# A four-layer graph network on one core: the identity moved into the adjacency, layernorm's last step and three other steps moved

## The chip, the cores and the metric

The kernel runs on one core of a Trainium2 chip. The time is the device time of one execution in microseconds; the runs of a kernel are given by their median. A core has a matrix engine (TensorE, PE in the profile, with its weight loads as PEld), a vector engine (VectorE, DVE), a scalar engine (ScalarE, ACT), a general one (GpSimd, POOL) and a queue engine that starts transfers (SyncE, SP). Each takes its instructions in order and waits for others by semaphores. ScalarE and GpSimd can start transfers too.

## The reference

`x` is 8 batches of 2048 nodes with 64 features, `adj` a 2048 x 2048 matrix of zeros and ones with ones on its diagonal. Four layers follow each other, each adds its input and normalizes:

```python
x = layernorm(x + hypergraph_attention(x, H, adj, ...))     # layer 0
x = layernorm(x + W1 . (dinv * (adj + I) * dinv) . x)       # layer 1
x = layernorm(x + chebyshev(x, E, adj, ...))                # layer 2: u1 = adj.x, u2 = adj.u1, u3 = softmax(relu(E.E^T)).x
x = layernorm(x + 3 steps of relu([v, adj.v].W31 + b31).W32 + b32)   # layer 3, on adj
```

Layer 1 alone uses `adj + I`, with `dinv` the inverse root of its row sums. `layernorm(r) = (r - mean) / sqrt(var + 1e-5)` over 64 features. E is the table of node embeddings, 2048 x 16.

## The kernel before

Two batches of 64 features make a pair of 128 columns: 4 pairs `p`, 16 node tiles `t` of 128, 4 chunks `c` of 512 nodes. The adjacency, transposed, stays in SBUF for the whole kernel as `adj[t][g]`, 16 row tiles in two column halves, in a rounded float type (fp32r) whose matmul takes one pass over 512 columns. A product with it takes `x` in two parts, a rounded one and the rest (`split`, line 161, makes `v0h`, `v0l` to `v3h`, `v3l` by chunk): 16 tiles x 2 parts x 4 chunks = 128 wide matmuls for a pair.

TensorE's order is written out by hand: `mm` and `transpose` pin each of its instructions (lines 170 to 174). The other engines' orders come from a scheduler that follows estimated times, so that an instruction issued earlier in the code can stand later in its engine's queue. Long products are generators, and `fill(n)` (line 370) takes n of their matmuls and puts them between the steps of a loop that has waits of its own. `later(n, f)` puts `f` on a list, and `tick()`, called once for each such matmul, runs it after n of them; the list is emptied from the front only.

The stages, in order: layer 0's prologue and attention, to about 230 us; its mixing loop (16 iterations over pairs and chunks: `mix_load`, `mix_ind`, `mix_g`, `mix_scores`, `mix_weigh`, `mix_end`), filled first with layer 0's products (`products`, tile `ug`), then with layer 1's (`layer1`, tile `u`); the rest of layer 1, which is `make_el` with the embedding's transposed table and plain product; the softmax support (`apt_tile`, tile `ua`) to about 805 us; layer 2's products and its weights (`py`) to about 1508 us; layer 3.

What the change and the steps of the prediction touch:

- `layernorm` (line 133): squares on ScalarE (line 148), a sum on VectorE (150), `var + eps` (152), the power on GpSimd (154), the last multiplication on VectorE (155).
- `mix_ind`: `pi` on TensorE, then `ind = pi * inv` on VectorE (line 809). `mix_scores`: four matmuls `pf` from `ind` and `gt`, four tanh on ScalarE (837), two differences on VectorE (839). `mix_weigh`: `pd`, a tanh, `ind` (851). `mix_end`: four transposes `pt`, the sum `r` (859), layernorm, a store to `x1_hbm` (863); then, for the first pair, the start of layer 1's parts.
- `mix_g` also loads `x` and adds it on GpSimd (line 825).
- `l1_parts` (line 868): loads `x1`, scales on GpSimd (870), splits. `l1_end` (line 873): `po`, `r = po * dinv` (880), `r += x1` on GpSimd (881), layernorm, and a store to `x2_hbm` (886) or, for the last pair, straight into `xn[3]`.
- `layer1`: beside each wide matmul on the chunk that holds tile `t`'s own nodes, one of 128 columns with the identity (`ident_r`) as its right-hand side adds the `I` of `adj + I`.
- `load_emb`, `make_el`, `make_er` (lines 979 to 1006): chunks of E in staged buffers `x` of which there are two, a plain product `pb`, and the rounded `el` and `er`.
- `first` (line 1230): for layer 3, transposes `x` into `h` (line 1211) and at once multiplies it by weights (`pr`) and splits it (`factor`).
- `finish` (line 1305): layer 3's last product `po`, the residual (1310), layernorm, two stores to the output (1313). Its layernorm keeps the squares in the `x` buffers, which `r` also uses.
- `check` (line 1327): in layer 3, 64 times a 128 x 512 piece of `adj` is loaded again into `fcav`, rounded on ScalarE (1330) and compared on VectorE (1331), to tell whether rounding changed anything. The next load waits for the comparison.

Of the kernel before, what the change touches and what calls it, by code (L numbers as in the profile page):

```python
# [56 lines left out]
def tile_gnn_fast(  # L57
# [23 lines left out]
    nc = tc.nc  # L81
# [51 lines left out]
    def layernorm(pool, r, dst, groups=2 * JT, centred=False, small=None, tag="ln_c", bufs=1):  # L133
# [21 lines left out]
        nc.vector.tensor_tensor(dst, xc, rstd[:, :, None].to_broadcast([P, groups, F]), ALU.mult)  # L155
# [38 lines left out]
    wrong = const.tile([P, 6], F32, name="wrong")  # L194
# [17 lines left out]
    def adj_c(t, c):  # L212

        return adj[t][c // 2][:, cols(c % 2)]

# [68 lines left out]

    places = {}
# [11 lines left out]
    def products():  # L297
# [40 lines left out]
        for p in range(NP):  # L338
            for g in range(2):
# [4 lines left out]
                for t in range(NT):  # L344
                    for i in range(2):
                        for c in own:
# [3 lines left out]
                            )  # L350
                            if t > 1:
                                next(turning, None)
# [3 lines left out]
                    if p + 1 < NP and t % JT == JT - 1:  # L356
# [3 lines left out]
                        if g == 1 and c < 2 or g == 0 and c >= 2:  # L360
                            fetch(p + 1, (c + 2) % NCH)
                for c in own:
# [399 lines left out]
    pending = []  # L762

    def later(n, f):

        pending.append([n, f])

    def tick():
        for e in pending:
            e[0] -= 1  # L770
        while pending and pending[0][0] <= 0:
            pending.pop(0)[1]()

# [19 lines left out]
    xn, done = [], [0] * NP  # L793
# [59 lines left out]
    def mix_end(i):  # L853
# [8 lines left out]
        layernorm(mp, grouped(r), grouped(r))  # L862
        nc.sync.dma_start(x1_hbm[p][:, wide(c), :], r)
        if p == 0:
            first_parts(c, mixed)

    def l1_parts(p, c):
        y = staged("y")
# [4 lines left out]
    def l1_end(p, c, ut):  # L873
# [8 lines left out]
        if p == NP - 1:  # L882
            layernorm(lp, grouped(r), grouped(xn[p][:, wide(c), :]), centred=True)
        else:
            layernorm(lp, grouped(r), grouped(r), centred=True)
            nc.sync.dma_start(x2_hbm[p][:, wide(c), :], r)
        done[p] += 1
        load_xn()
# [8 lines left out]
    def layer1(p):  # L897

        for g in range(2):
            own = (2 * g, 2 * g + 1)  # L900
            ug = None
            for t in range(NT):
# [5 lines left out]
                for i in range(2):  # L908
                    for c in own:
                        end = t == NT - 1 and i == 1  # L910
                        half = part[p, t // JT][i][:, t % JT, :]
                        mm(
                            u[c], lhsT=half, rhs=adj_c(t, c),
                            start=t == 0 and i == 0, stop=end and t // JT != c,
                        )
# [28 lines left out]
    for i in range(steps + 1):  # L944
        k = 10 if i > NCH else 8
# [17 lines left out]
    load_xn()  # L963
# [20 lines left out]
    def load_emb(c):  # L984

        et = flat_x("et")
# [3 lines left out]
    ets = [load_emb(c) for c in range(2)]  # L990

    def make_el(c):
        et = ets.pop(0)
# [11 lines left out]
        if c + 2 < NCH:  # L1005
            ets.append(load_emb(c + 2))

    for c in range(NCH):
# [46 lines left out]
    for i, (c, t) in enumerate(order_ct):  # L1055
# [4 lines left out]
        for p in range(NP):  # L1060
# [3 lines left out]
            if t == NT - 1 and p % 2:  # L1064
                for q in (p - 1, p):
# [3 lines left out]
                    else:  # L1069
                        nc.scalar.copy(raws[c, q], ug[p // 2][:, q % 2, :])  # L1070
        if t == 1 and c > 0:
            apt_end(c - 1)
        if t == 8 and c + 1 < NCH:
            make_er(c + 1, load_emb(c + 1))
# [155 lines left out]
    def first(c, where):  # L1230
        h[c] = first_h(0, c, l2.tile([P, C], F32, tag=f"{where}{c}", name=f"h{c}"))
        factor(c, h[c], bd_e, None)
# [4 lines left out]
    for p in range(NP):  # L1237
        for c in range(NCH):
            r = staged("r").rearrange("p t (b f) -> p t b f", f=F)
            for b in range(2):  # L1240
                a_z = xg[b]
                for j in range(JT):
# [27 lines left out]
    for c in (2, 3):  # L1270
        first(c, "g")
# [33 lines left out]
    def finish(p, c, h):  # L1305
# [13 lines left out]
    left = l2.tile([P, NT, NCH], F32, tag="m", name="left")  # L1319
# [830 lines left out]
```

## Time and profile before

| what | value |
|---|---|
| median of 3 runs | 1989.77 us (1988.22 to 1994.02) |
| the profiled execution | 1991.48 us |
| its span, first to last instruction | 1989.7 us |
| mean granted TensorE clock | 0.98 |
| TensorE busy, 300 to 400 us | 93.10 of 100 |
| TensorE busy, 400 to 500 us | 87.88 of 100 |
| TensorE busy, 500 to 600 us | 90.16 of 100 |
| TensorE busy, 600 to 1400 us | 99.4 to 100 of each 100 |
| TensorE busy, 1900 to 1990 us | 72.23 of 90 |
| VectorE, GpSimd busy, 300 to 400 us | 53.46 and 43.22 of 100 |

A page of the profile gives each engine's busy time, the span in 40 slices, the chain of work that ended last and the costliest groups of instructions. In the groups, `u<-adj,v0h` is a tile written and the tiles read, followed by the shapes. In the order of time, a row is the start in us, the duration, the engine, the line, the operation, the tiles and the count; in brackets is how long the engine had stood idle before it and what ended that. Times of matmuls overlap, since the array takes the next while one ends. A wide product with fp32r operands is one record, a plain fp32 matmul two.

### The profile page before, as it was taken

The numbers are of one execution on the slowest core, as the hardware profiler recorded it, in microseconds if no ns is written. First come the engines' busy times: TensorE is split into PE (matmuls) and PEld (weight loads), VectorE is DVE, ScalarE is ACT, GpSimd is POOL, SyncE is SP. The second block draws the span as 40 slices with busy tenths as digits, with TensorE's granted clock in tenths as the row PEclk, the third lists the DMA queues.
The fourth block names the chain that finished last, engine by engine and source line by source line (L and its number), as shares of the span: only waits on it lengthen the run. The fifth ranks groups of instructions, "written<-read, shape, count | busy, mean of one in ns | idle before, by whom it ended". The sixth has DMA issues, their size and how long they took to land.

```text
span 1989.7 us, 19780 instructions
## 1 busy us (share of the span) xinstructions
PE 1887.9 (95%) x7228; PEld 1230.2 (62%) x7228; DVE 978.2 (49%) x1660; ACT 397.0 (20%) x771; POOL 519.8 (26%) x464
## 2 busy tenths in 40 slices
PE   6889899889899999999999999999999999999996
PEld 4667566556654444755665575565446777877775
DVE  6679555555422211357556736655784342332422
ACT  1445343333222111100000000000002221212211
POOL 3678643544354344311001101100001020100101
PEclk9899899989999999999999999999999999999998
DMA  9833334332400000311101110110101121211201
GB/s 310 292 105 100 130 122 143 117 110 84 154 16 27 4 24 21 118 37 53 51 35 43 56 50 32 58 49 33 46 25 40 38 64 43 59 43 48 54 22 23
DMA packets 94186, 143.12 MB, mean 72 GB/s; under 512 B 29232, under 2 KB 40112, under 8 KB 93696
## 3 DMA queue, kind: packets, MB, share of 16 engines
q1 hardware_dynamic: 84448, 105.52, 16.8%
q0 software_dynamic: 7760, 27.66, 4.3%
q10 hardware_dynamic: 1872, 8.59, 1.1%
q8 instruction: 59, 0.97, 0.2%
q14 instruction: 47, 0.39, 0.1%
HBM read 98.67 MB, written 43.06 MB: 71 GB/s over the span
## 4 chain that ended last, share of the span: by engine, by line
PE 72%; DMA 6%; DVE 5%; POOL 3%; issue 3%; ACT 2%; SPq 0%; POOLq 0%; ACTq 0%; DVEq 0%
PE u L171 29%; PE py L171 21%; PE ua L171 11%; PE ug L171 3%; DMA fcav<-in_adj_t 3%; POOL ln_r L154 2%; PE pr L171 2%; PE pf L171 2%; DVE fcav L1331 1%; POOL r L881 1%; PE s L171 1%; PE pt L174 1%; DVE ln_v L150 1%; PE po L171 1%; DMA x_hbm<-r 0%
## 5 line engine op out<-in xcount | busy, mean ns | idle before, releaser
L171 PE MATMUL py<-wp,xg 128*128 128x512 f32 x1024 | 476.9, 594 | 0.6 <-DMA xg<-u_hbm 0.6
L171 PEld LDWEIGHTS py<-wp,xg 128*128 128x128 f32 x1024 | 193.9, 190 | 162.4 <-issue 140.0
L1250 DVE TENSOR_TENSOR fcav<-py,emb_n 128x512 f32<-128x512 f32 x256 | 177.0, 691 | 136.9 <-PE py L171 130.4
L171 PE MATMUL ua<-pt,xn 128*128 128x512 f32 x512 | 230.2, 592 | 1.4 <-DVE pt L1034 1.4
L154 POOL TENSOR_TENSOR ln_r<-ln_e,neg_half 128x8 f32<-128x8 f32 x64 | 106.4, 1662 | 458.7 <-DVE ln_e L152 420.5
L1251 DVE TENSOR_REDUCE r<-fcav 128x32 f32<-128x512 f32 x256 | 175.6, 686 | 8.2
L171 PEld LDWEIGHTS ua<-pt,xn 128*128 128x128 f32 x512 | 97.0, 190 | 110.8 <-issue 104.2
L171 PE MATMUL u<-adj,v0h 128*128 128x512 f32 x384 | 149.6, 455 | 0.8 <-ACT h L1394 0.8
L171 PE MATMUL u<-adj,v2h 128*128 128x512 f32 x384 | 144.2, 440 | 0.0
L171 PE MATMUL u<-adj,v2l 128*128 128x512 f32 x384 | 142.0, 433 | 0.0
L171 PE MATMUL u<-adj,v1h 128*128 128x512 f32 x384 | 139.6, 431 | 0.0
L171 PE MATMUL u<-adj,v0l 128*128 128x512 f32 x384 | 139.5, 429 | 0.0
L171 PE MATMUL u<-adj,v3l 128*128 128x512 f32 x384 | 139.5, 428 | 0.0
L171 PE MATMUL u<-adj,v1l 128*128 128x512 f32 x384 | 139.1, 429 | 0.0
L171 PE MATMUL u<-adj,v3h 128*128 128x512 f32 x384 | 138.8, 429 | 0.0
L1034 DVE TENSOR_SCALAR pt<-pt 128x512 f32<-128x512 f32 x64 | 31.4, 491 | 150.7 <-ACT pt L1033 150.4
L1039 POOL TENSOR_TENSOR acc<-acc,pt 128x512 f32<-128x512 f32 x60 | 76.7, 1279 | 103.9 <-DVE pt L1034 103.2
L1331 DVE SCALAR_TENSOR_TENSOR fcav<-fcav,ar 128x512 f32<-128x512 f32 x64 | 48.4, 756 | 97.5 <-ACT ar L1330 97.5
L171 PEld LDWEIGHTS u<-adj,v0h 128*128 128x128 f32 x384 | 71.0, 189 | 36.7 <-issue 24.3
L171 PEld LDWEIGHTS u<-adj,v2l 128*128 128x128 f32 x384 | 73.5, 192 | 27.5 <-issue 13.4
L171 PEld LDWEIGHTS u<-adj,v1l 128*128 128x128 f32 x384 | 71.2, 189 | 30.4 <-issue 16.5
L171 PEld LDWEIGHTS u<-adj,v2h 128*128 128x128 f32 x384 | 72.0, 192 | 29.2 <-issue 16.2
(361 smaller groups left out, 2679.8 us busy)
## 6 DMA issues: line engine op xcount, KB each, us to landing
adj<-in_adj_t POOLq DMA_DIRECT2D x32, 512.0 KB, 7.3
fcav<-in_adj_t SPq DMA_DIRECT2D x64, 256.0 KB, 2.9
u_hbm<-ut SPq DMA_DIRECT2D x48, 256.0 KB, 2.7
xg<-u_hbm SPq DMA_DIRECT2D x96, 128.0 KB, 2.8
x_hbm<-r SPq DMA_DIRECT2D x28, 256.0 KB, 2.2
hs_hbm<-st ACTq DMA_DIRECT2D x8, 584.0 KB, 5.8
xt<-in_x_t SPq DMA_DIRECT2D x16, 256.0 KB, 5.7
ut<-u_hbm SPq DMA_DIRECT2D x16, 256.0 KB, 3.5
```

The costliest lines, as they stand in the source:

```text
L150: nc.vector.tensor_reduce(var, squares, AX.X, ALU.add)
L154: nc.gpsimd.tensor_tensor(rstd, vare, neg_half[:, :groups], ALU.pow)
L171: tc.keep_in_program_order(nc.tensor.matmul(*args, **kw))
L174: tc.keep_in_program_order(nc.tensor.transpose(dst, src, ident))
L881: nc.gpsimd.tensor_tensor(r, r, x1, ALU.add)
L1034: nc.vector.tensor_scalar(pt, pt, 1.0, None, op0=ALU.max)
L1039: nc.gpsimd.tensor_tensor(accs[c], accs[c], pt, ALU.add)
L1250: nc.vector.tensor_tensor(pr, py, e_b, ALU.mult)
L1251: nc.vector.tensor_reduce(r[:, j, b, cols(k, OH)], pr, AX.X, ALU.add)
L1331: nc.vector.scalar_tensor_tensor(seen_a, seen_a, 1.0, ar.bitcast(F32), op0=ALU.mult, op1=ALU.not_equal, accum_out=left[:, t, k:k + 1],)
```

## The change

Layer 1's identity matmuls go. Instead, at the end of layer 0's last pair, the identity is added onto the 16 diagonal blocks of `adj` on GpSimd, eight after each half of that product, and subtracted again on VectorE in the first chunk of the softmax support, a block for each tile. The check of `adj` gets a further comparison for the 16 blocks, that adding and subtracting gives the same value; and it writes into its own copy, not over the loaded piece. Layernorm hands its last multiplication to its caller, which in layers 0 and 1 puts it off by 7 matmuls together with the store behind it; `l1_parts` waits for a store that isn't issued yet. `fill` takes 9 matmuls where it took 10. E's four chunks are loaded at once into `xn[3]`, ahead of the loads of `xn`, with 32 matmuls before they are used. `first` puts its product off by 2, 8 or 12 matmuls. The last half of layer 3 starts `finish` 6 matmuls after its chunk, not 14; its squares lie in the `ut` buffers; and the very last store starts on ScalarE.

```diff
@@ layernorm
-    def layernorm(pool, r, dst, groups=2 * JT, centred=False, small=None, tag="ln_c", bufs=1):
+    def layernorm(pool, r, dst, groups=2 * JT, centred=False, small=None, tag="ln_c", bufs=1, put_off=None):
...
-        nc.vector.tensor_tensor(dst, xc, rstd[:, :, None].to_broadcast([P, groups, F]), ALU.mult)
+
+        def end():
+            nc.vector.tensor_tensor(dst, xc, rstd[:, :, None].to_broadcast([P, groups, F]), ALU.mult)
+
+        (put_off or (lambda f: f()))(end)
@@ next to adj_c
+    def onto_diagonal(t, eng, op):
+
+        block = adj_c(t, t // JT)[:, cols(t % JT, P)]
+        eng.tensor_tensor(block, block.bitcast(F32), ident, op)
@@ products (pending, later and tick now stand before it)
+                            tick()
...
+                if p == NP - 1:
+
+                    for t in range(g * NT // 2, (g + 1) * NT // 2):
+                        onto_diagonal(t, nc.gpsimd, ALU.add)
@@ mix_end
-        layernorm(mp, grouped(r), grouped(r))
-        nc.sync.dma_start(x1_hbm[p][:, wide(c), :], r)
-        if p == 0:
-            first_parts(c, mixed)
+
+        def end(f):
+            f()
+            nc.sync.dma_start(x1_hbm[p][:, wide(c), :], r)
+            stored.add((p, c))
+            if p == 0:
+                first_parts(c, mixed)
+            elif (p, c) in due:
+                l1_parts(p, c)
+
+        layernorm(mp, grouped(r), grouped(r), put_off=lambda f: later(7, lambda: end(f)))
 
     def l1_parts(p, c):
+
+        if (p, c) not in stored:
+            due.add((p, c))
+            return
@@ l1_end
+        def end(f):
+            f()
+            if p < NP - 1:
+                nc.sync.dma_start(x2_hbm[p][:, wide(c), :], r)
+            done[p] += 1
+            load_xn()
+
+        dst = xn[p][:, wide(c), :] if p == NP - 1 else r
+        layernorm(lp, grouped(r), grouped(dst), centred=True, put_off=lambda f: later(7, lambda: end(f)))
@@ layer1
-                        if t // JT == c:
-                            mm(u[c][:, cols(t % JT, P)], lhsT=half, rhs=ident_r, start=False, stop=end)
-                            tick()
-                            yield
@@ the mixing loop and what follows it
-        k = 10 if i > NCH else 8
+        k = 9 if i > NCH else 8
...
+    while len(stored) < steps:
+        fill(1)
     mix_scope.close()
     xnp = ctx.enter_context(tc.tile_pool(name="xnp", bufs=1, side="right"))
     xn += [xnp.tile([P, NT, P], F32, name=f"xn{p}") for p in range(NP)]
-    load_xn()
...
-    ets = [load_emb(c) for c in range(2)]
+
+    ets = [load_emb(c, xn[NP - 1][:, wide(c), :].rearrange("p t f -> p (t f)")) for c in range(NCH)]
+
+    load_xn()
...
-        if c + 2 < NCH:
-            ets.append(load_emb(c + 2))
-
+
+    fill(32)
@@ the softmax support
+        if c == 0:
+            onto_diagonal(t, nc.vector, ALU.subtract)
@@ first and its callers
-        factor(c, h[c], bd_e, None)
+        later(n, lambda: factor(c, h[c], bd_e, None))
...
-                        first(j - 1, "g")
+                        first(j - 1, 2)
...
-        first(c, "g")
+        first(c, 4 * c)
@@ finish
-        layernorm(va, grouped(r), grouped(r), centred=True, small=l2, tag="x", bufs=2)
+        layernorm(va, grouped(r), grouped(r), centred=True, small=l2, tag="ut", bufs=2)
         for b in range(2):
-            nc.sync.dma_start(
+            (nc.scalar if b and p == NP - 1 and c == NCH - 1 else nc.sync).dma_start(
@@ check
-            seen_a, seen_a, 1.0, ar.bitcast(F32), op0=ALU.mult, op1=ALU.not_equal,
+            ar.bitcast(F32), seen_a, 1.0, ar.bitcast(F32), op0=ALU.mult, op1=ALU.not_equal,
             accum_out=left[:, t, k:k + 1],
         )
+        if t // JT == k:
+
+            block = seen_a[:, cols(t % JT, P)]
+            one, two, same = (ar[:, cols(i, P)] for i in range(3))
+            nc.vector.tensor_tensor(one, block, ident, ALU.add)
+            nc.vector.tensor_tensor(two.bitcast(F32), one.bitcast(F32), ident, ALU.subtract)
+            nc.vector.scalar_tensor_tensor(
+                same.bitcast(F32), two.bitcast(F32), 1.0, block, op0=ALU.mult, op1=ALU.not_equal,
+                accum_out=left_d[:, t:t + 1],
+            )
@@ layer 3's loop
-                            later(14 + 8 * k, lambda c=c, h=h[c], p=p: finish(p, c, h))
+                            at = 6 if very_end else 14 + 8 * k
+                            later(at, lambda c=c, h=h[c], p=p: finish(p, c, h))
```

More of the change, by code (lines that the diff above doesn't have):

```diff
@@ L193, in tile_gnn_fast @@
     MIX = 2 * P + 2 * F + 2
-    wrong = const.tile([P, 6], F32, name="wrong")
+    wrong = const.tile([P, 7], F32, name="wrong")
     nc.vector.memset(wrong, 0.0)
@@ L283, in load_x, with later, tick @@
             tc.keep_in_program_order(load)
+    pending = []
+    def later(n, f):
+        pending.append([n, f])
+    def tick():
+        for e in pending:
+            e[0] -= 1
+        while pending and pending[0][0] <= 0:
+            pending.pop(0)[1]()
     places = {}
@@ L757, in tile_gnn_fast @@
     hy_scope.close()
[L762 to L772, printed above, removed]
     lp_scope = ExitStack()
@@ L792, in tile_gnn_fast @@
     uts, invs, gts, inds, tts, rs = {}, {}, {}, {}, {}, {}
-    xn, done = [], [0] * NP
+    xn, done, stored, due = [], [0] * NP, set(), set()
     steps = NP * NCH
@@ L881, in l1_end @@
         nc.gpsimd.tensor_tensor(r, r, x1, ALU.add)
[L882 to L887, printed above, removed]
-        load_xn()
+        def end(f):
[6 more added lines that the diff above has]
+        layernorm(lp, grouped(r), grouped(dst), centred=True, put_off=lambda f: later(7, lambda: end(f)))
     def load_xn():
@@ L909, in layer1 @@
                     for c in own:
-                        end = t == NT - 1 and i == 1
-                        half = part[p, t // JT][i][:, t % JT, :]
-                        mm(
-                            u[c], lhsT=half, rhs=adj_c(t, c),
-                            start=t == 0 and i == 0, stop=end and t // JT != c,
+                        mm(
+                            u[c], lhsT=part[p, t // JT][i][:, t % JT, :], rhs=adj_c(t, c),
+                            start=t == 0 and i == 0, stop=t == NT - 1 and i == 1,
                         )
@@ L962, in tile_gnn_fast @@
     xn += [xnp.tile([P, NT, P], F32, name=f"xn{p}") for p in range(NP)]
-    load_xn()
     def flat_x(name):
@@ L982, in make_er, with load_emb @@
         nc.vector.tensor_tensor(er[c][F:P, :], et[F:P, :], er[c][F:P, :], ALU.subtract)
-    def load_emb(c):
-        et = flat_x("et")
+    def load_emb(c, et):
         nc.sync.dma_start(et, emb_4[:, cols(c)])
         return et
-    ets = [load_emb(c) for c in range(2)]
+    ets = [load_emb(c, xn[NP - 1][:, wide(c), :].rearrange("p t f -> p (t f)")) for c in range(NCH)]
+    load_xn()
     def make_el(c):
-        et = ets.pop(0)
+        et = ets[c]
         nc.scalar.copy(el[:, cols(c)], et)
@@ L1073, in tile_gnn_fast @@
         if t == 8 and c + 1 < NCH:
-            make_er(c + 1, load_emb(c + 1))
+            make_er(c + 1, load_emb(c + 1, flat_x("et")))
         if t == 8 and c == 1:
@@ L1228, in tile_gnn_fast, with first @@
     h = [None] * NCH
-    def first(c, where):
-        h[c] = first_h(0, c, l2.tile([P, C], F32, tag=f"{where}{c}", name=f"h{c}"))
-        factor(c, h[c], bd_e, None)
+    def first(c, n):
+        h[c] = first_h(0, c, l2.tile([P, C], F32, tag=f"g{c}", name=f"h{c}"))
+        later(n, lambda: factor(c, h[c], bd_e, None))
     for b in range(2):
@@ L1319, in tile_gnn_fast @@
     left = l2.tile([P, NT, NCH], F32, tag="m", name="left")
+    left_d = l2.tile([P, NT], F32, name="left_d")
     checks = [(t, k) for t in range(NT) for k in range(NCH)]
@@ L1339, in check @@
             nc.vector.tensor_reduce(wrong[:, 4:5], left.rearrange("p t k -> p (t k)"), AX.X, ALU.add)
+            nc.vector.tensor_reduce(wrong[:, 6:7], left_d, AX.X, ALU.add)
             nc.vector.tensor_reduce(total, wrong, AX.X, ALU.add)
```

## The prediction

> **What bounds the kernel now.** I read the totals first, then the chain of waits, then TensorE's waits, and last the order of time in the places where it waited. From the page:
>
> ```profile
> PE 1887.9 (95%) x7228; PEld 1230.2 (62%) x7228; DVE 978.2 (49%) x1660; ACT 397.0 (20%) x771; POOL 519.8 (26%) x464
> PEclk9899899989999999999999999999999999999998
> ```
>
> TensorE has work for all but about 100 us of 1989.7. From 562 to 1480 us it is never free for more than a moment; so a change pays only if it takes instructions off TensorE, or fills a hole before 562, near 1490, or in the last 30 us. TensorE's waits, over the whole span, name the holes (us in total, times, longest):
>
> ```profile
> PE pf L171 <- DVE ind L809: 13.8, 4, 4.1
> ...
> PE pb L171 <- DMA et<-in_emb: 6.4, 1, 6.4
> ...
> PE pt L174 <- ACT t L837: 4.8, 3, 2.7
> ...
> PE pr L171 <- ACT h L1211: 2.6, 3, 1.2
> PE pr L171 <- DVE h L1214: 2.2, 1, 2.2
> PE po L171 <- ACT ut L926: 2.0, 2, 1.3
> ```
>
> One of the four waits of `pf`, in order of time (start, duration, then what):
>
> ```profile
> 363.23 2.07 POOL L154 TENSOR_TENSOR ln_r<-ln_e,neg_half 128x8 f32<-128x8 f32 x1 [2.13 <-DVE ln_e L152]
> ...
> 365.33 1.52 DVE L155 TENSOR_TENSOR r<-r,ln_r 128x512 f32<-128x512 f32 x1 [1.54 <-POOL ln_r L154]
> ...
> 366.78 0.68 DVE L809 TENSOR_TENSOR ind<-pi,inv 128x512 f32<-128x512 f32 x1
> ...
> 367.51 2.08 PE L171 MATMUL pf<-ind,fcav 64*128 64x512 f32 x4 [4.06 <-DVE ind L809]
> 369.38 1.91 PE L171 MATMUL pf<-gt,fcav 64*128 64x512 f32 x4
> ```
>
> VectorE stands in layer 1's layernorm at line 155, which waits for GpSimd's power; `ind`, which the next matmuls need, stands behind it.
>
> **What the Trainium skill says.** "TensorE: Matmul & The Clock Gate", Part 1 (the HAM clock gate): after an idle window of about 3.4 us the array runs at half its clock, until it has been busy about as long. The trace agrees: the eight `pf` records above take 3.78 us in the chain of waits, 1.92 where nothing was missing before them (420.10). A hole thus costs more than its length. "Perfetto Trace Analysis", Tensor Engine Instruction: a matmul's end is estimated, so I price matmuls from start to start. "Advanced Engine Details and Errata", GPSIMD Details: GpSimd shares an interface with VectorE where that reads two SBUF inputs; line 155 takes 1.52 us beside GpSimd's `y`, 0.69 elsewhere. "DMA: Bandwidth & Descriptors", Issuing engines are not separate DMA queues: a second issuing engine saves only issue time.
>
> **1. The identity matmuls go.** Layer 1 has 4 pairs x 4 chunks x 4 tiles x 2 halves = 128 of them. The by-line mean is 220 to 257 ns each (29.8 us in all), but the starts say less:
>
> ```profile
> 515.68 0.63 PE L171 MATMUL u<-adj,v3h 128*128 128x512 f32 x2
> 516.15 0.22 PE L171 MATMUL u<-ident_r,v3h 128*128 128x128 f32 x1
> 516.21 0.68 PE L171 MATMUL u<-adj,v3l 128*128 128x512 f32 x2
> 516.72 0.22 PE L171 MATMUL u<-ident_r,v3l 128*128 128x128 f32 x1
> ...
> 533.93 0.62 PE L171 MATMUL u<-adj,v2h 128*128 128x512 f32 x2
> 534.39 0.63 PE L171 MATMUL u<-adj,v2l 128*128 128x512 f32 x2
> ```
>
> Two wide matmuls and one of these take 0.579 us (4.05 us over seven periods from 516.15), two wide ones alone 0.467. So each costs 0.112 us, and all 128 give **14.3 us** (29.8 at most, if the records' own length were right). What replaces them is off TensorE: 16 additions of 128x128 on GpSimd at the end of layer 0's last pair, 16 subtractions on VectorE in the apt stage. The trace has no such GpSimd row; a quarter of line 881's 1.29 us to the whole of it, 0.32 to 1.29, I take 0.45: 3.6 us for each half, on an engine 43% busy from 300 to 400 us. The first half is covered by 64 matmuls (15 us) of the second half, the second by layer 1's first 64. In the built order they stand among GpSimd's mixing work, at the eighth iteration or so; nothing there to 3 us of delay once. The subtractions, at 0.23 us (line 1284, 128x128), wait in VectorE's queue for layer 1's last reads; behind them stand `v2l` and `v3l` of the last pair, needed 8 and 12 tiles (7 to 11 us) later: nothing.
>
> **2. Layernorm's last step is put off** by 7 matmuls. Alone this would change little, since `fill` runs 8 or 9 of them before `ind` is issued. But the built order shows the scheduler placing much differently: before, `ind` stands right behind layer 1's line 155 or one reduction after it in four iterations, the four waits of the trace; after, that is so in the first case and, behind two line 155s, in one later. GpSimd's residual sum for layer 1, which stood behind the sum waiting for an x load, comes ahead of it in more cases. The holes of this stage are 13.8 + 4.8 us, and the slow clock behind the four `pf` holes another 5.8 (3.78, 3.38, 3.79 and 2.56 in the chain against 1.92 each): 24.4. With `fill` at 9 for 10, TensorE also arrives a little earlier at what it waits for. I take half back, **12 us**; 0 to 22 as ends.
>
> **3. E in x's place.** All four loads of E are issued at once, into the last xn, behind the last `x1` store on SP; before, the third waited for a staged buffer and collided with the two 1 MB loads of xn. The hole is 6.4, plus 0.3 before the second `pb`, plus 2.3 of slow clock behind it (509.2 to 513.0 takes 3.8 us for what is 1.5 at full clock). In the built order the first `pb` now comes 37 wide matmuls and a `po` after the last `pt`: 10.3 us. Against that: VectorE, ScalarE and GpSimd need about 7.5 us to the last store (line 859 and after, 0.68 + 0.69 x 5 + 0.63 + 0.17 + 1.65, and queueing), issues 0.4 and the load 2.9: near 11. On ScalarE the two xn issues, which wait for that store to land (2.2), stand ahead of `v3h` and of the copy that the second `po` needs, and `v3h`'s own load stands on SP behind E's four. So I expect 3 to 5 us of new holes at `pb` and `po` for 9 + 2 removed: **5 us**, between -4 and 9.
>
> **4. Factors put off.** `pr` follows `pt` at once at the end of layer 2; its holes are 2.6 + 2.2, and the matmuls behind the first take 5.30 us instead of 3.44: 6.7. After, two `py` groups (3.4 us) lie between, and the copies were ready 2.65 us after `pt`. **6 us**, 3 to 7.
>
> **5. Tail.**
>
> ```profile
> 1975.18 0.69 DVE L1310 TENSOR_TENSOR r<-po,xn 128x512 f32<-128x512 f32 x1
> 1977.96 0.63 ACT L148 ACTIVATE ln_c<-r 128x512 f32<-128x512 f32 x1 [5.38 <-DMA out_x<-r]
> 1981.32 0.69 DVE L155 TENSOR_TENSOR r<-r,ln_r 128x512 f32<-128x512 f32 x1 [1.81 <-POOL ln_r L154]
> ```
>
> The squares wait for an output store, since they share its buffers; in `ut`'s they don't. `po` ends at 1973.8; then 0.71 + 0.65 + 0.72 + 0.30 + 1.75 in the same steps put the last line 155 at about 78.0 instead of 81.3: 3.3. The last store from a second queue saves one issue, 0.4. **3.7 us.**
>
> **6. Checks.** Sixteen of 64 get three more VectorE steps, near 0.75 us (0.23 each and a read-out of 0.08), before the next load may start. One turn is 2.9 + 0.63 + 0.76, 4.35 us, so three fill 13 of a group's 16.6; with one such check, 13.8. ScalarE's `h` stands behind the check's copies, and in the last step of each pair the turns already run late (1594.81 to 1627.91 in the chain). The stores' waits on ScalarE go. I take **1 us lost**, 6 lost to 3 won.
>
> Sum: 14.3 + 12 + 5 + 6 + 3.7 - 1 = 40. The profiled execution took 1991.5 us for a span of 1989.7; the median of the runs, 1989.8, happens to equal the span. So **1950** for the median.
>
> **Rivals.** (a) The mixing stage stays paced by VectorE and GpSimd: shorter fills only lengthen `pf`'s wait, E's hole returns at `po`. Then half of the identities (7), 6, 3.7 and 1 remain: **1972**. For it: `ind`'s operand was ready 9 us before TensorE wanted it, and it was the in-order queue that held it. Against: half of the bad placements are gone. (b) All holes of parts 2 to 4 close with their slow clock: 14.3 + 24.4 + 11 + 6.7 + 3.7, **1930**. Against: `fill` covers about 2.1 us at a time, layernorm needs over 5. (c) Slower: the checks' serial turn becomes the bound of layer 3, since ScalarE is strictly in order and `h` stands behind the copies. It decides once a turn exceeds a third of a group, 16.6 / 3 = 5.5 us on average; the estimate is 4.35 + 0.75 x 16/64 = 4.5. At 6.4 a group is 2.6 us late, over 20 groups 52 us: **2002** with the other savings. (d) The identities aren't removed: the built order excludes it (TensorE has just 128 fewer).
>
> **Numbers.** Forecast 0.62 (own range 1937 to 1963), (a) 0.22, (b) 0.11, (c) 0.05. Within 0.3% (6 us, what a measurement can tell) ends of part 2 and 3 together with (c)'s beginnings leave 0.01. Faster 0.94, same 0.01, slower 0.05. The range reaches into (a) and (b): 1933 to 1970.
>
> **What would show it.** No `ident_r` rows with `u`, two wide matmuls every 0.467 us throughout layer 1; `pf <- ind` under 8 us in total; `pb` and `po` waits under 5 us; no `pr` waits near 1490; no `ln_c` waiting for `out_x`. The prediction is wrong if the stage from 320 us to the first `ua` shortens by less than 20 us, if the `po` or `pf` waits grow, or if `h` in layer 3 waits for `ar` longer than before.

## The result, and the profile after

| | before | after |
|---|---|---|
| median | 1989.44 us (1988.22 to 1994.02, 4 runs) | 1979.32 us (1976.23 to 1981.15, 4 runs) |
| profiled execution, its span | 1991.48, 1989.7 us | 1976.23, 1974.4 us |

The ratio is 0.9943, with a 95% interval of 0.9923 to 0.9964. The forecast was 1950, and its range ended at 1970: the sign was right, the size was a quarter of what was expected.

The profiled execution is the fastest of its four, so its 15 us overstate the median's 10. Of these 15, 3.5 lie before 230 us, where the first `pi` starts (233.5 before, 230.0 after). That start lies anywhere from 228.8 to 236.2 us in the runs below, and at 236.2 in one whose code up to there is that of the kernel before (e14); nothing is read from it.

Totals and clock, from the page of the changed kernel:

```profile
PE 1870.6 (95%) x7100; PEld 1214.4 (62%) x7100; DVE 1001.6 (51%) x1741; ACT 394.6 (20%) x771; POOL 530.7 (27%) x480
PEclk9999899899899999999999999999999999999998
```

The 128 instructions are gone from TensorE. Its waits over the whole span (us in total, times, longest):

```profile
PE po L175 <- ACT ut L948: 20.5, 4, 8.6
...
PE pt L178 <- DVE ind L865: 5.0, 1, 5.0
PE pf L175 <- DVE ind L823: 4.3, 2, 3.9
...
PE pb L175 <- DMA xn<-in_emb: 3.2, 1, 3.2
...
PE pf L175 <- DVE r L905: 2.7, 1, 2.7
```

`pf`'s wait for `ind` fell from 13.8 to 4.3 us and `pb`'s from 6.4 to 3.2; `pr`'s two lines are gone. In their place `po` waits 20.5 us for `ut`, where it waited 2.0, and two waits of mixing are new, `pt`'s 5.0 and `pf`'s 2.7 for `r`. Between the first `pi` and the first `ua` TensorE is busy for 283.5 us where it was 294.5, and idle for 45.4 where it was 34.2: what the missing identities freed went into waiting. By stage, from the starts of matmuls in the profiled executions:

| stage | before | after | gain | forecast |
|---|---|---|---|---|
| mixing and layer 1: first `pi` to first `ua` | 328.7 | 329.0 | -0.3 | 31 |
| softmax support: first `ua` to first `py` | 292.3 | 292.7 | -0.4 | 0 |
| layer 2's weights: first `py` to last | 648.0 | 642.1 | 5.9 | 6 |
| layer 3: first `po` to last | 368.8 | 365.5 | 3.3 | -1 |
| tail: last `po` to the span's end | 16.2 | 13.0 | 3.2 | 3.7 |

The forecasts are those of the prediction's steps 1 to 3, none, 4, 6 and 5. From the last `py` to the first `po` both take 102.2 us. So one stage holds the whole miss. The longest of its holes, in order of time:

```profile
436.81 0.32 SPq L879 DMA_DIRECT2D x_hbm<-r  x1
439.00 0.33 SPq L290 DMA_DIRECT2D r<-in_x_n  x1
439.43 0.38 SPq L894 DMA_DIRECT2D y<-x_hbm  x1
441.71 1.26 POOL L839 TENSOR_TENSOR r<-r,gn 128x512 f32<-128x512 f32 x1 [5.65 <-DMA r<-in_x_n]
...
444.15 1.04 POOL L895 TENSOR_TENSOR y<-y,dinv 128x512 f32<-128x512 f32 x1
445.23 0.62 ACT L170 CAST v3h<-y 128x512 fp32r<-128x512 f32 x1 [7.85 <-POOL y L895]
...
446.33 1.06 ACT L948 COPY ut<-u 128x512 f32<-128x512 f32 x2
446.96 2.08 PE L175 MATMUL po<-bd_w,ut 128*128 128x128 f32 x8 [8.60 <-ACT ut L948]
```

Read upwards: `po` needs `ut`; ScalarE copies it only after casting the next pair's last piece, `v3h`; that needs `y` from GpSimd, where `y` stands behind the sum of an `x` load; and on SP both loads wait for one store. In the program's order that store is the very x1 chunk that `y` loads: layer 1 has caught up with mixing and asks for a chunk that is only just finished. The kernel before has the same order, but there `v3h` (381.54, 453.33) waited for nothing at the first two pairs' ends:

```profile
453.33 0.61 ACT L166 CAST v3h<-y 128x512 fp32r<-128x512 f32 x1
454.58 1.06 PE L171 MATMUL po<-bd_w,ut 128*128 128x128 f32 x8
```

Its `y` was ready at 451.06, only 2.3 us ahead of the cast. Counted from the first `pi`, TensorE wants this `po` after 208.3 us in the changed kernel and after 221.1 in the kernel before; `y` is ready after 215.2 and 217.6. TensorE comes 12.8 us earlier, `y` only 2.4. Two more such holes lie at 376.03 (2.35 us) and 519.37 (7.49 us). Behind each long one the clock is low: from 510 to 520 us the granted clock is 0.50, and the `po` above takes 2.08 us where the others take 1.05.

### The profile page after: what moved, and what is told of

It is laid out like the page before. It is cut to its first block, busy times and chain, and to the rows that moved or that the text cites. A ratio compares the mean times of both kernels' runs of the same rounds, so it can differ in the third digit from the quotient of the medians.

```text
span 1974.4 us, 19582 instructions
## 1 busy us (share of the span) xinstructions
PE 1870.6 (95%) x7100; PEld 1214.4 (62%) x7100; DVE 1001.6 (51%) x1741; ACT 394.6 (20%) x771; POOL 530.7 (27%) x480
## 4 chain that ended last, share of the span: by engine, by line
PE 76%; DVE 4%; DMA 4%; POOL 4%; issue 3%; ACT 1%; SPq 1%; POOLq 0%; DVEq 0%; ACTq 0%
PE u L175 32%; PE py L175 22%; PE ua L175 11%; PE ug L175 3%; PE pr L175 2%; POOL ln_r L154 2%; PE po L175 1%; PE pf L175 1%; PE pt L178 1%; PE s L175 1%; DMA x<-x_hbm 1%; POOL r L906 1%; DMA r<-in_x_n 1%; DMA x_hbm<-r 1%; PE pd L175 0%
## 5 line engine op out<-in xcount | busy, mean ns | idle before, releaser
L1358 DVE SCALAR_TENSOR_TENSOR ar<-fcav,ar 128x512 f32<-128x512 f32 x64 | 45.4, 709 | 109.1 <-ACT ar L1357 109.1
L175 PEld LDWEIGHTS u<-adj,v3l 128*128 128x128 f32 x384 | 72.0, 188 | 29.4 <-issue 14.9
```

Of the source, the lines that this page charges most:

```text
L175: tc.keep_in_program_order(nc.tensor.matmul(*args, **kw))
L1358: nc.vector.scalar_tensor_tensor(ar.bitcast(F32), seen_a, 1.0, ar.bitcast(F32), op0=ALU.mult, op1=ALU.not_equal, accum_out=left[:, t, k:k ...
```

## The experiments

"Stage" below is mixing and layer 1, first `pi` to first `ua`, in the one profiled execution; a ratio is that of the times of all runs to the kernel before, with its 95% interval. Executions of one kernel differ: e3's 17 runs span 1975.81 to 1987.95. So the stage says where time went, the ratio how much. From the first `py` to the last it takes 641.9 to 642.1 us in every run with the change's `first`, and 646.0 to 648.1 in every run with the old one. That isn't all gain: one more group of `pr` now runs behind the last `py`, and there `u` waits for `v2l`, 1.2 us in the changed kernel and 2.2 to 2.9 in the other fourteen runs with its `first`, a wait that no run with the old one has. Up to layer 3's first `po` it is 744.2 to 747.5 us with the new `first` and 748.2 to 750.3 with the old, 3 us on the mean. From layer 3's first `po` to its last 365.5 to 365.9 with the squares in `ut`, 367.9 to 371.3 with the squares in `x`.

### The first four: what makes `po` wait

**e1**, layernorm's end at once:

```diff
-    put_off=lambda f: later(7, lambda: end(f)))
+    put_off=end)
```

> The changed kernel, but layernorm's last product, the store and what follows it are issued at once, in mixing and in layer 1 (not seven matmuls later); the rest of the change stays. Theory A (the store of x1 now comes late, y behind it on SP comes late, and the ScalarE copies that po needs stand behind the cast of y): po's wait for ut, 20.5 us in the changed kernel, falls below 6; pf's and pt's waits of the kernel before (13.8 and 4.8) come back in part; mixing and layer 1 take 315 to 326 us (329.0 in the changed kernel), the whole 1962 to 1976. Theory B (PE, freed of the identities, reaches po earlier and ScalarE's order alone makes it wait): po's wait stays at 15 to 25 and pf's wait is added to it: 1980 to 1992. Theory C (the loads of E and xn delay y): only the last of the three holes, 7.5 us, changes, or none.

Ratio 0.9959 (0.9944 to 0.9973), stage 331.3 us. `po` waited 22.6 us for `ut`, not less. Theory A falls: the lateness isn't made by the putting off. B comes nearest (median 1983.05). And `pf` waits only 4.1 us for `ind` here too: what took its wait down from 13.8 isn't the putting off either.

**e2**, the copies ahead of the cast, by moving `l1_parts(p + 1, NCH - 1)` behind the copies and keeping both in program order:

```diff
-                if g == 1 and p + 1 < NP and t % JT == JT - 1:
+                if g == 1 and p + 1 < NP and t % JT == JT - 1 and t < NT - 1:
                     l1_parts(p + 1, t // JT)
...
-                nc.scalar.copy(ut, u[c])
+                tc.keep_in_program_order(nc.scalar.copy(ut, u[c]))
                 later(6 + 8 * k, lambda p=p, c=c, ut=ut: l1_end(p, c, ut))
+            if g == 1 and p + 1 < NP:
+                l1_parts(p + 1, NCH - 1)
```

> The changed kernel, but layer 1's last cast of the next pair's y stands behind the two copies of u on ScalarE (in the program, and held in that order). Theory A and B both say that po's wait for ut falls from 20.5 to below 4 us. A, with a size: no other wait takes its place, the clock recovers too, mixing and layer 1 fall from 329.0 to 304 to 313 us, the whole to 1952 to 1962. Theory D (the lateness is y's, and whoever needs it waits: the next pair's first group needs v3h and v3l): u's wait for v3l or a copy stuck behind v3l appears with 10 to 20 us, and the whole is 1968 to 1978.

Ratio 0.9902 (0.9878 to 0.9926), stage 319.4 us. The median, 1971.92, misses A and lies in D, but D's wait isn't there: in this stage `u` waits for neither `v2l` nor `v3l`. `po` waits 8.6 us, 6.9 of it at 533.6, where the copy stands on ScalarE behind the third load of `xn` (532.27), which follows a store of layer 1's result. The hole in the middle is gone; in the same place as above, ScalarE and TensorE have:

```profile
440.80 1.09 ACT L948 COPY ut<-u 128x512 f32<-128x512 f32 x2
445.08 0.62 ACT L170 CAST v3h<-y 128x512 fp32r<-128x512 f32 x1 [3.19 <-POOL y L895]
...
441.45 1.16 PE L175 MATMUL po<-bd_w,ut 128*128 128x128 f32 x8
```

`po` starts 3.6 us before the cast of `v3h` does. But `pf`'s wait for `ind` is 8.1 us again instead of 4.3: part of the time went there. The order on ScalarE is a cause of the holes, and not the only one.

**e3**, the identity alone: from the change only `onto_diagonal`, its two callers, the loss of the identity matmuls, the new check, and 9 for 10.

> The kernel before with one part of the change: the identity added onto the adjacency in place, its 128 matmuls left out, subtracted again in the next stage and the test of the diagonal blocks, with stretches of 9 matmuls in place of 10 (the same number of wide ones, nearly). Theory A: layernorm at once keeps y in time, so po's wait stays below 6, pf's and pt's stay as before (13.8 and 4.8), and the 14.3 us of the matmuls are gained in full: 1972 to 1978. Theory B: po's wait rises to 15 to 25 us and eats the gain: 1984 to 1992. Theory E (the GpSimd additions and VectorE subtractions are not hidden): a wait of PE for pt in the stage after layer 1, or for v0 to v3 casts in front of it, of 5 us or more.

Ratio 0.9961 (0.9951 to 0.9970), stage 318.4 us in a profile of the fastest of its 17 runs, 7 us below their median. `po` waits 11.9 us for `ut`, with no putting off in the kernel, where the kernel before waited 2.0. `pf` falls to 7.6 over its three releasers. Removing the identity matmuls, with 9 for 10, is enough to open the hole at `po`, between A's 6 and B's 15; of the 14.3 us a gain of 7.8 is left by the ratio. No wait for the GpSimd or VectorE additions is seen (theory E).

**e4**, `k = 10` in place of 9 in the changed kernel.

> The changed kernel with stretches of 10 matmuls of layer 1 between the steps of mixing, as before, in place of 9. All 10 are now wide, so layer 1 advances faster against mixing. Theory A: layer 1 asks for y earlier than mixing has stored x1, so y comes later still against its user: po's and u's waits together are 20 to 35 us: 1972 to 1985. Theory B (a shorter stretch is what exposes the wait): they fall below 10 us, the whole to 1960 to 1968.

Ratio 0.9983 (0.9971 to 0.9994), stage 337.2 us:

```profile
PE po L175 <- ACT ut L948: 16.6, 3, 7.4
PE u L175 <- ACT v3h L170: 11.3, 1, 11.3
```

27.9 us together, as theory A had it, though the median, 1989.37, is above its 1985: more layer 1 for each step of mixing makes it worse, where theory B had it better. Of theory A this much stays: layer 1 asks for `y` before mixing has it.

### The next four: putting off and E

**e5**, E loaded and staged as in the kernel before (the hunks of `load_emb` and `make_el` undone, and `fill(32)` with them).

> The changed kernel with E loaded as the kernel before loads it: two chunks at once into the two buffers named x, two more once those are used, and no stretch of 32 matmuls ahead of pb. The runs so far: mixing and layer 1 take 328.7 us in the kernel before, 329.0 in the changed one and 318.4 with the identity alone, so the other two edits of this stage lose about 10.6. Theory F (E's four loads ahead of the last y on SP, next to the two loads of 1 MB for xn, make that y late and so the last po): the hole of 7.5 at po for ut goes, pb's wait for E stays at 2 to 6, the stage takes 317 to 322 and the whole 1963 to 1970. Theory A (putting layernorm off is what loses): the stage stays at 326 to 330, the whole at 1974 to 1980.

Ratio 0.9916 (0.9890 to 0.9942), stage 319.1 us against 329.0. The waits and the stage are those of theory F; the median, 1972.05, is 2 above its range, and the intervals of e5 and of the changed kernel overlap. How E's edit gives its hole back can be read in the changed kernel (SP, ScalarE, GpSimd, TensorE):

```profile
504.46 2.06 SPq L1009 DMA_DIRECT2D xn<-in_emb  x4
506.56 0.74 SPq L894 DMA_DIRECT2D y<-x_hbm  x1
...
504.61 0.81 ACTq L923 DMA_DIRECT2D xn<-x_hbm  x2
518.21 0.62 ACT L170 CAST v3h<-y 128x512 fp32r<-128x512 f32 x1 [14.48 <-POOL y L895]
...
517.14 1.04 POOL L895 TENSOR_TENSOR y<-y,dinv 128x512 f32<-128x512 f32 x1 [14.05 <-DMA y<-x_hbm]
...
519.37 2.08 PE L175 MATMUL po<-bd_w,ut 128*128 128x128 f32 x8 [7.49 <-ACT ut L948]
```

The last `y` is issued behind E's four loads and beside two loads of 1 MB, and is there for GpSimd 10.6 us after its issue; the copy that `po` needs stands behind its cast. But theory F's reason isn't shown: in e5 GpSimd starts on this `y` at 521.46, 4.3 us later than here, and `po` doesn't wait for it, since both copies (509.48, 509.95) stand ahead of the cast (522.53). What ended the hole is again the order on ScalarE, which the scheduler made differently.

**e6**, the loads of xn written behind the use of E's chunks, E's place kept:

```diff
+    held = {0}
...
-            if xn and done[p] == NCH:
+            if xn and not held and done[p] == NCH:
...
-    load_xn()
-
     def make_el(c):
...
         make_el(c)
         fill(16)
+    held.clear()
+    load_xn()
```

> The changed kernel, with the loads of xn (three of 1 MB on ScalarE's queue) held back until E's four chunks have been used; E stays in xn's place and ahead of y on SP. Theory F1 (it is the bytes: 2 MB of xn share the DMA engines with E and y): the hole of 7.5 us at po and pb's 3.2 shrink to below 3 together, the stage takes 316 to 321 and the whole 1962 to 1969. Theory F2 (it is the order on SP alone: y behind E): po's hole stays at 5 to 8, the stage at 325 to 330. If xn comes too late for the stage after, PE waits at ua or at the casts of xn for 3 us or more.

Ratio 0.9918 (0.9894 to 0.9942), stage 323.8 us: between the two. In the built order only one of the two early loads moved: the first still starts at 506.86, right behind E's first, the second at 519.23. `pb` waits 3.1 us, and `po` 4.7 at another place, at 537.0, where the copy stands behind the third load of xn (535.96), as in e2. The hole behind `v3h` is gone, but here too both copies stand ahead of that cast. So e6 doesn't tell the bytes from the order on SP.

**e7**, the kernel before with the putting off alone.

> The kernel before with one part of the change: layernorm's last product, the store and what follows put off by seven matmuls, in mixing and in layer 1. The identity matmuls, stretches of 10 and E's loads stay as before. The prediction's step: pf's and pt's holes (13.8 and 4.8 us) and the slow clock behind them shrink, mixing and layer 1 fall from 328.7 to 312 to 322, the whole to 1974 to 1984. Theory G (pf's holes come from the length of the chain of VectorE, ScalarE and GpSimd through one step of mixing, not from the order of VectorE's queue): holes of the same sum, at pf or elsewhere, 325 to 331 for the stage, 1986 to 1994 for the whole.

Ratio 0.9993 (0.9977 to 1.0010): no gain clear of 3 us of noise. The stage is 324.6 us in the profile; `pf` waits 9.4 us, where it waited 13.8, `pt` 7.2 where it waited 4.8. Part of the wait moved from one consumer to the next.

**e8**, e2 and e6 together.

> The changed kernel with both repairs: the copies of u ahead of the last cast of y, and xn's loads held back until E's chunks are used. If the two losses add (the hole at po in the middle of the stage, from the order on ScalarE; the one at its end, from the transfers): the stage takes 308 to 315 us and the whole 1955 to 1963. If mixing's own chain paces the stage (theory G), the second repair adds little to the first: 317 to 320 and 1966 to 1972.

Ratio 0.9898 (0.9880 to 0.9917), stage 318.5 us: nothing added to e2 (as in e6, the first load of xn still starts beside E's, at 504.25). At this point mixing's own chain seemed to set the pace (theory G).

### Is it mixing's chain?

**e9**, e2 with stretches of 8 throughout:

```diff
-        k = 9 if i > NCH else 8
+        k = 8
```

> The kernel with the copies first (e2), with stretches of 8 matmuls of layer 1 between mixing's steps from first to last, in place of 9. About 46 wide matmuls, 10.7 us, leave the loop of mixing for the stretch behind it. Theory G (from the moment layer 1 runs beside it, mixing is paced by its own chain over VectorE, ScalarE, GpSimd and SP): the loop, first pi to last, stays at 229 to 234 us (232.6), PE's holes in it grow by 8 to 11, and the whole is 1976 to 1984. Rival (PE paces it, with chance holes): the loop falls to 222 to 226 and the whole stays at 1968 to 1974. For layer 1 catching up with mixing: po's wait for ut is no more than in e2 (8.6).

Ratio 0.9869 (0.9850 to 0.9887), stage 312.0 us. The loop, first `pi` to last, fell from 232.6 to 211.4: 21.2 us, with 38 wide matmuls (8.9 us) fewer in it. Theory G would have left it as it was, and the rival had allowed only the 10.7. The casts of `v3h` at the first two pairs' ends follow the copies at once, with no wait. Two holes are left at `po`, 8.0 and 6.1 us; ahead of the first, ScalarE has:

```profile
472.58 0.81 ACTq L923 DMA_DIRECT2D xn<-x_hbm  x2
473.44 1.07 ACT L948 COPY ut<-u 128x512 f32<-128x512 f32 x2 [6.67 <-issue]
```

The copy stands behind two loads of xn, which start only at 472.58, after mixing's last store (470.23).

**e10**, e1 with no layer 1 beside mixing from the sixth step on:

```diff
-        k = 9 if i > NCH else 8
+        k = 0 if i > NCH else 8
+        if i == NCH + 1:
+            for _ in remaining:
+                pass
```

> The changed kernel with layernorm at once (e1), with no layer 1 matmuls between mixing's steps from the sixth on: layer 1 runs whole behind mixing. Only the length of a step of mixing is asked, from pi to pi; it is 12.5 us with 32 wide matmuls of the first stage beside it, 13.45 with 36, and 18 on the mean (13 to 25) once layer 1 runs. Theory G in its strict form (mixing's own chain is as long as that): 14 to 18 us. Rival H (the chain alone is shorter, and layer 1's ends, casts, loads and stores in the same queues of VectorE, GpSimd, ScalarE and SP make it longer): 8 to 12.5.

From `pi` to `pi` a step takes 8.6 to 12.2 us, 10.25 on the mean (333.43 to 405.18, seven steps), against 18.7 in the changed kernel (336.44 to 467.23). Rival H holds, and with e9 theory G is ruled out: mixing alone could go much faster. (As a whole this kernel took 2011.34 us in one run, since TensorE is empty in mixing.)

**e11**, the changed kernel with layer 3's squares back in the buffers named `x`.

> The changed kernel with layer 3's squares of layernorm in the buffers named x again, in place of ut. If these buffers are what layer 3 gained by: from the first po of layer 3 to the last 368 to 371 us (365.5 in the changed kernel and in all runs with its layer 3, 367.9 to 371.1 in those with the old one), the whole 3 us longer than the changed kernel, ratio 0.995 to 0.997. If the gain came from the last steps or the test in its new form: 365.5, and no difference.

Ratio 0.9956 (0.9939 to 0.9972); too near the changed kernel's to tell by the clock. The profile tells: `po` to `po` 368.0 us instead of 365.5, and the tail 16.2 instead of 13.0, with the old wait back in ScalarE's order of time:

```profile
1971.64 0.63 ACT L148 ACTIVATE ln_c<-r 128x512 f32<-128x512 f32 x1 [5.36 <-DMA out_x<-r]
```

So without this change of a buffer's name both gains of layer 3 are gone; that it makes them alone, without the earlier `finish` and the store on ScalarE, no run shows.

**e12**, e2 and e5, with `fill(24)` more ahead of mixing's last transposes and of the first `pb`.

> The changed kernel with the copies of u ahead of the last cast (e2), E loaded as before (e5), 24 matmuls of layer 1 ahead of the last transposes of mixing and 24 more ahead of the first pb. If the losses found are separate: the holes at pt (5.0) and pb (2 to 3) go below 1.5 each, the stage of mixing and layer 1 takes 308 to 314 us and the whole 1957 to 1965. If layer 1's matmuls moved there are then missing later (layer 1 waits for the last y): the stage stays at 317 to 320, the whole at 1966 to 1972.

Ratio 0.9941 (0.9924 to 0.9959), stage 323.7 us: a miss. `pt`'s 5.0 went, but `pb` then waited 8.9 us for E and `po` 7.6 for `ut`. Holes filled one by one at a pace that doesn't fit only move.

### The pace

A pair of layer 1 is 128 wide matmuls. At 9 for each of the four stretches of a step, that is 3.6 steps of mixing, while mixing takes 4 steps to make a pair: layer 1 gains on it until it meets the last `y`. At 8 it is 4.0 steps.

**e13**, the changed kernel with `k = 8`, nothing else.

> The changed kernel with stretches of 8 matmuls throughout, and nothing else (ScalarE's order as the change has it). Theory I (layer 1 at 36 matmuls a step catches up with mixing, and only then the order on ScalarE matters): the casts of v3h wait for nothing at the first two pairs' ends, mixing and layer 1 take 310 to 316 us as in e9 (312.0), the whole 1961 to 1967. Rival (both are needed): po waits 12 us or more for ut behind v3h, the stage 318 to 326, the whole 1969 to 1977.

Median 1956.97 us (1951.05 to 1958.52), ratio 0.9813 (0.9782 to 0.9844), stage 304.4 us. ScalarE at the first two pairs' ends:

```profile
373.43 0.62 ACT L170 CAST v3h<-y 128x512 fp32r<-128x512 f32 x1 [1.42 <-PE u L175]
...
436.34 0.62 ACT L170 CAST v3h<-y 128x512 fp32r<-128x512 f32 x1 [1.28 <-POOL y L895]
```

and TensorE's waits:

```profile
PE pb L175 <- issue: 6.2, 1, 6.2
PE pf L175 <- DVE ind L823: 5.8, 2, 3.4
...
PE pt L178 <- ACT t L851: 4.2, 2, 2.1
...
PE po L175 <- ACT ut L948: 1.9, 2, 1.1
```

7.60 and 7.85 us of waiting for `y` became 0 and 1.28, and `po`'s 20.5 became 1.9. The `y` that was loaded 2.6 us after its store (436.81, 439.43) now follows it by 9.0 us (421.82, 430.84): layer 1 no longer asks for a chunk that is only just finished. TensorE's idle time in the stage falls from 45.4 to 25.7 us. One digit is worth 24.6 us of the stage, more than the order on ScalarE, the transfers and the putting off together.

**e14**, the kernel before with 9 in place of 10.

> The kernel before with stretches of 9 in place of 10, nothing else. A pair of layer 1 is 144 matmuls there with its 16 identities, so 9 make 4.0 steps of mixing per pair, as 8 do without them; 10 make 3.6. Theory I: the same catching up holds the kernel before, so its pf holes (13.8) shrink below 7 and mixing and layer 1 fall from 328.7 to 314 to 322 us, the whole to 1975 to 1984. Rival (the kernel before was at its best pace, and v3h never waited there at the first two ends): the stage 327 to 334, the whole 1989 to 1996.

Ratio 1.0029 (1.0019 to 1.0039), stage 328.5 us. Theory I fails for the stage. It holds for the loop: from the first `pi` to the last it falls from 231.4 to 214.7 us, with 7.4 us of layer 1's matmuls fewer in it, nearly to the 211.4 to 212.9 of the runs with 8 and no identities. But from the last `pi` to the first `ua` it takes 113.7 us instead of 97.3, and TensorE idles 17.3 of it instead of 12.9. TensorE's waits, the first three from 345 to 420 us, the next three to 485, the last to 562:

```profile
PE pf L171 <- DVE r L880: 2.7, 1, 2.7
PE pf L171 <- ACT th L850: 2.0, 2, 1.5
PE pt L174 <- ACT t L837: 1.2, 1, 1.2
...
PE pt L174 <- DVE ind L851: 4.9, 2, 4.7
PE pd L171 <- DVE t L839: 4.3, 2, 2.6
PE pf L171 <- DVE ind L809: 1.6, 1, 1.6
...
PE pb L171 <- DMA et<-in_emb: 5.4, 1, 5.4
```

`pf`'s do fall below 7 (6.3), but `pt` has 6.1 and `pd` 4.3; `pb`'s 5.4 was 6.4 before. So the count of steps per pair tells how long the loop is, and not what becomes of the stage: the matmuls that the loop no longer takes must find a place behind it without new holes. In e15, with E as before, that part takes 100.7 us, in e13 and e17 92.2 and 91.3.

**e15**, e3 with `k = 8`.

> The kernel before with the identity alone (e3), with stretches of 8. Mixing and layer 1 took 318.4 us with 9. Theory I: 303 to 312 us, the whole 1965 to 1972 (the later parts of the change, worth some 10 us, are not in it). Against e13 it tells what putting off and E's place do at this pace: if they are worth nothing, the stage is no longer here than in e13; if putting off does what the prediction said, it is longer here by 5 us or more.

Ratio 0.9903 (0.9878 to 0.9928), stage 312.8 us, 15.9 less than the kernel before, with TensorE idle for 33.4 us of it (34.2 before): with the pace changed from 10 to 8 beside it, the loss of the identity matmuls is worth about what they cost. Against e13 the stage is 8.4 longer; 5.6 of TensorE's waiting is one hole at `po`, whose copy stands behind the third load of xn (522.46).

**e16**, e8 with `k = 8`.

> e9 (stretches of 8, copies ahead of the last cast) with the loads of xn held back until E's chunks have been used. e9 has two holes left, 8.0 and 6.1 us, both at po for ut; ahead of the first the copies stand behind two loads of xn on ScalarE's queue, which wait for mixing's last store. If that is it, the first hole goes (below 2), the stage falls from 312.0 to 300 to 307 and the whole to 1950 to 1958. If another wait takes its place, 310 to 314 and 1960 to 1966.

Median 1953.54 us (1953.21 to 1956.26), ratio 0.9806 (0.9781 to 0.9832), stage 304.2 us. The 8.0 us hole of e9 is gone, as it should be if the xn loads ahead of the copies on ScalarE's queue made it: here `po` runs at 468.6, and the first load of xn starts at 473.86. `pb` waits 5.6 instead. It is the lowest median of all, but not to be told from e13, which has neither repair: e9's two holes don't arise in e13's order.

### Two last ones

**e17**, e1 with `k = 8`.

> e13 (the changed kernel with stretches of 8) with layernorm's last product, the store and what follows at once. If the 8.4 us between e15 (312.8 us for mixing and layer 1) and e13 (304.4) are E's place alone: 303 to 307, whole ratio 0.980 to 0.984. If they are the putting off: 311 to 315, ratio 0.985 to 0.988.

Ratio 0.9824 (0.9808 to 0.9840), stage 304.2 us: the putting off is worth nothing at this pace either, and the 8.4 us are E's place with the 32 matmuls ahead of it. TensorE's busy time from 485 to 530 us fits: 44.7 of 45 in e13, 44.0 here, 37.1 in e15 with E staged as before, and 29.4 in the changed kernel. I read it so that both are needed, E's place and the matmuls that 8 leaves for after the loop to lie over the loads; no run shows the second by itself, and in e18 still more are left, and `pb` waits longer.

**e18**, `k = 7` from the sixth step on.

> The changed kernel with stretches of 7 from the sixth step on. A step of mixing has then 28 wide matmuls, and a pair of layer 1 takes 4.6 of them. If the pace that fits is 4.0 steps a pair: PE's holes in the loop grow by as much as the matmuls leave it, the stage is 308 to 316 us, the whole 1960 to 1968. If the loop is still bound by PE at 28: the stage stays at 302 to 306, the whole at 1952 to 1958.

Ratio 0.9861 (0.9845 to 0.9877), stage 310.7 us, in the range of a pace that is best near 8. The loop is only 4.6 us shorter than e13's (207.6 against 212.2) for some 10 us of matmuls taken out, and `pb` waits 10.4 us for E.

## Why the prediction was wrong

- **Step 1, the identities (14.3).** Right as a price: no row of `u` with the identity is left, and two wide matmuls start every 0.467 us in layer 1:

```profile
366.64 0.63 PE L175 MATMUL u<-adj,v3h 128*128 128x512 f32 x2
367.11 0.62 PE L175 MATMUL u<-adj,v3l 128*128 128x512 f32 x2
367.57 0.63 PE L175 MATMUL u<-adj,v3h 128*128 128x512 f32 x2
```

  At a pace of 8 the stage shortens by 15.9 us (e15, where the pace differs too). As a gain in this kernel it was wrong: alone it brought 7.8 us by the ratio (e3). The covers were right: GpSimd's additions take 0.46 us each by their median (0.45 taken), VectorE's subtractions 0.28 (0.23 taken), and TensorE waits for neither.
- **Step 2, the putting off (12, 0 to 22).** Here the prediction failed. It took 12 us of TensorE's holes back; instead TensorE's idle time in the stage grew by 11.2 us (34.2 to 45.4). The putting off is worth nothing that the runs can tell (e7, e17). `pf`'s wait did fall from 13.8 to 4.3 us, but it falls as far without the putting off (4.1 in e1, 3.9 in e3). The failing sentence is "With `fill` at 9 for 10, TensorE also arrives a little earlier at what it waits for": it stands among the gains and has no price of its own, and of the waits that an earlier arrival meets only mixing's were looked at. TensorE, freed of the identities, came 12.8 us earlier to `po`, whose copies stood behind a `y` that came 2.4 us earlier, and `po`'s wait grew from 2.0 to 20.5 us; with 8 for 9 it is 1.9, and the stage is 24.6 us shorter (e13). The trace of before had the warning: the copies already stood behind `v3h` on ScalarE, with `y` ready 2.3 us ahead.
- **Step 3, E (5, -4 to 9).** The risk was named with its place, the xn issues and `v3h` ahead of the copy, and `v3h`'s load behind E's four. With 9 these held and the gain was lost (e5: 9.9 us of stage in the profile, not certain in the medians); with 8 the gain is 8.4 (e15, e17). The first lies outside the bounds of this term, the second near their upper end.
- **Steps 4 and 5 (6 and 3.7).** 5.9 and 3.2 in the profile. For `first` the 5.9 are in part luck: the new wait of `u` for `v2l`, which the prediction doesn't have, is short in this execution, and over all runs 3 us are left. The 0.4 us for the last store's second queue isn't seen: e11, which keeps that queue, has the tail of the kernel before, 16.2. In the tail the squares start 0.78 us after the residual, where they stood 5.38 us idle for a store:

```profile
1961.73 0.69 DVE L1336 TENSOR_TENSOR r<-po,xn 128x512 f32<-128x512 f32 x1 [3.04 <-PE po L175]
1962.51 0.63 ACT L148 ACTIVATE ln_c<-r 128x512 f32<-128x512 f32 x1 [2.03 <-DVE r L1336]
...
1965.88 0.69 DVE L157 TENSOR_TENSOR r<-r,ln_r 128x512 f32<-128x512 f32 x1 [1.81 <-POOL ln_r L154]
```

- **Step 6, the checks (-1, between -6 and 3).** The sign was wrong: layer 3 gained 3.3 us, of which 2.5 go with the squares' buffers (e11). The longer checks cost TensorE nothing: it is busy 100.00 of each 100 us from 1600 to 1900, 98.8 to 99.1 before.
- **Rivals.** (a), 1972, was near in number and named `po` as the place where E's hole returns; its mechanism, a stage paced by VectorE and GpSimd where shorter fills only lengthen a wait, is refuted by e9 and e13: with 8.9 us of matmuls fewer in it, the loop is 21.2 and 25.0 us shorter. (b) has the holes closing, and they grew. (c), the checks as a bound, didn't occur.

The own sum for all parts was 40 us. With one digit changed the kernel is 37 us faster than the kernel before on the same chip, by the ratio of 0.9813. That the two are near is in part luck: at that pace the putting off brings 0 for 12, E 8.4 for 5, layer 3 some 3 for -1.

What stays open: what the order of E and `y` on SP and the bytes of xn cost by themselves, since in e5 and e6 the order on ScalarE changed as well; and whether the kernel before would gain by 9 with E in its new place.

## What to carry to other kernels

When work is taken off the engine that bounds a stage, two streams that share it change their relative pace: count how many steps of one pass per unit of the other, before and after, and look at what the faster one now has to wait for, and at where the work goes that the loop no longer takes (e14). A filler's length is then a parameter to be measured again, by one step each way, before any hole is repaired by hand. And a copy that the matrix engine needs should not stand, on an in-order engine, behind a cast whose operand comes from memory.

## What was not expected of the hardware

Between executions the point where mixing starts moved by 6.5 us in runs whose code up to there is the changed kernel's (228.8 in e9, 235.3 in e10), and one kernel's times over 12 (e3, 17 runs), while another's stayed within 1.8 (e2, only 4 runs): a single profile can't carry a difference of a few microseconds between two kernels. An instruction that only starts a transfer held its queue like any other: before two loads of xn ScalarE stood 6.67 us, and the copies of 1.07 us behind them came so late that TensorE stood 7.98 (e9); the holes of 6.9 us in e2 and 4.7 in e6 have the same form. And the array was slow behind a hole of 2.81 us too, shorter than the 3.4 us in the prediction: in the kernel before, the eight `pf` at 403.23 take 3.38 us instead of 1.92.
